# Router logits of two token blocks on VectorE instead of TensorE, in a fused Mamba, MLP and mixture-of-experts kernel

## The chip, the cores and the metric

The kernel runs on one core of one Trainium2 chip. The metric is the device time of one execution in microseconds (us). A core has five engines that work side by side, each with its own queue of instructions, issued in a fixed order: TensorE (PE in the profile; PEld is its loading of weights), VectorE (DVE), ScalarE (ACT), GpSimd (POOL) and SyncE (SP), which here only starts transfers (DMAs). An instruction waits for semaphores of others, and what stands behind it on the same engine waits with it.

## What is computed

The reference takes 2048 tokens of 512 numbers, in float32. A layer norm, an RMS norm, a Mamba-2 layer and an MLP of width 2048 with residuals come first. Then a mixture of experts works on the layer-normed rows; of that part this is what matters here:

```
x = x + attn_and_mlp(layernorm(x))
n = layernorm(x)                                   # (2048, 512)
router_logits = n @ Wr                             # Wr: (512, 8)
topk_w, topk_idx = top_k(softmax(router_logits), 2)
combine = topk_w / sum(topk_w), spread over the 8 experts
y[e] = (silu(n @ Wg[e]) * (n @ Wu[e])) @ Wd[e]     # Wg, Wu: (512, 352), Wd: (352, 512)
out = x + sum over e of combine[e] * y[e]
```

## The kernel before

Tokens lie in 16 tiles of 128 rows. The Mamba layer goes through them in 8 steps of 256 tokens, the MLP (`feed_forward(fb)`) in 4 blocks of 512 tokens, `fb` 0 to 3, each with 16 chunks `c` of 128 hidden channels. From the third Mamba step on, the program interleaves the MLP of one block with the Mamba layer of a later one; the third block's MLP ends after the Mamba layer, and the last block's MLP (`feed`, from 1065 us) runs with the third block's routing and with the loading of all experts' weights into SBUF. Then come the expert tiles.

**The order.** From the third Mamba step on, a region called `manual_schedule` holds PE to the order in which the Python program emits its instructions. The order on the other engines, SP's queue of loads too, is laid down by a scheduler when the kernel is built, by priorities and by its own idea of times; on the chip it is fixed. Generators cut the work into pieces, and each `yield` is a place at which the emitting program goes over to another generator. In the loop over `feed` (`for n in range(4 * NFC)`) four steps make one chunk, and the third step of each chunk (`n % 4 == 2`) is followed by one piece of the routing of block 2 and then of the first table. In the loop over the expert tiles two pieces come with each tile, taken from the routing of block 3 and then from the second table.

**Buffers.** A tile that is allocated with a `tag` shares that tag's `bufs` buffers with all others of the tag, and its first writer waits until one is free. `mid` (3 buffers of 512 numbers for each partition) serves the routing; `mg` (3) and `md` (4) hold MLP weights; `row` (5) the rows of a block; `h2T` one transposed block. In PSUM, `tr`, `g`, `u` and `d` have two banks each from the last block's MLP on.

**The weights of the MLP.** For each chunk SP loads `mg` (L534), `ms` (L547) and `md` (L552); the experts' weights come by L924, L926 and L927. Each waits for its buffer in SP's queue.

**Routing a block** (`route`). When the block's MLP has ended, `normed(j)` writes the normed rows `xn` of tile `j` (L598) and stores them to DRAM in `xnd` (L599), and for blocks 0 to 2 also in `xnd1` (L601), from where the expert tiles gather them later. PE turns each tile of `xn` with four transposes (L201), ACT copies the result to `xT` (L203), and PE multiplies it with the router weights (L607):

```
xT = mid([NK, P], f"xT{fb}_{j}")
transposed(xn, xT)
...
nc.tensor.matmul(pl, xT[:, k, :], wr_sb[:, k, :], start=(k == 0), stop=(k == NK - 1))
```

DVE copies the logits to `lg` (L608) and, when all four tiles are there, picks the two best experts (`chosen`, `both`), their weights, and the counts `prior` of earlier tokens (L627 to L650). Two pieces later PE counts positions with the matmul `pr` (L654, L655), which reads `both` and `prior`, and GpSimd scatters token numbers and weights into `lists` (L669).

**Expert tiles.** `table` makes from `lists` which expert and which tokens each tile of 128 places has. The first table has `NS1` tiles, all full, from blocks 0 to 2 alone; the second has the rest. For tile `s`, GpSimd gathers rows (L1026), PE transposes them and multiplies with the expert's weights (L1045), DVE makes `eh` (L1050) and copies its transpose to `ehT` (L1059), PE multiplies again (L1066), DVE weighs the rows (L1071) and GpSimd adds them to `out` in DRAM (L1072). Rows are fetched up to two tiles ahead.

Of the kernel before, what the change touches and what calls it, by code (L numbers as in the profile page):

```python
# [9 lines left out]
F32 = mybir.dt.float32  # L10
I32 = mybir.dt.int32
AF = mybir.ActivationFunctionType
ALU = mybir.AluOpType
# [3 lines left out]
P = 128  # L17
T = 2048
D = 512
NK = D // P  # L20
# [8 lines left out]
NFB = T // FB  # L29
# [5 lines left out]
NE = 8  # L35
# [3 lines left out]

NS = (2 * T + NE * (P - 1)) // P  # L40

NS1 = 10


NSA = (2 * T + NE * (P // 2)) // P
# [6 lines left out]


@with_exitstack
def mamba_mlp_moe(ctx, tc, x, w_in, w_out, w_gu, w_down, par, wr, wg, wu, wd, out):

    nc = tc.nc

    def bc(ap, axis, n):
        ap = ap.unsqueeze(axis)
        shape = list(ap.shape)
        shape[axis] = n
        return ap.to_broadcast(shape)
# [7 lines left out]
    pmlp = ctx.enter_context(tc.tile_pool(name="pmlp", bufs=2, side="right"))  # L73
    wk = ctx.enter_context(tc.tile_pool(name="wk", bufs=2, side="right"))
# [21 lines left out]
    def load_w_in(pair):  # L96
# [15 lines left out]
        out=tri, in_=ones, pattern=[[1, P]], compare_op=ALU.is_ge, fill=0.0, base=0, channel_multiplier=-1  # L112
# [3 lines left out]
        out=late, in_=ones, pattern=[[-1, P]], compare_op=ALU.is_gt, fill=0.0, base=0, channel_multiplier=1  # L116
# [16 lines left out]
        out=upto, in_=ones[:, : NE * NE].rearrange("p (e f) -> p e f", e=NE), pattern=[[1, NE], [-1, NE]],  # L133
# [27 lines left out]
    xnd = scratch.tile([T + P, D], F32, name="xnd", tag="xnd")  # L161
# [15 lines left out]
    def bank(kind, shape, name):  # L177
        pool, tag = use[kind]
        return pool.tile([P, *shape], F32, name=name, tag=tag)
# [17 lines left out]
    def transposed(src, dst, weight=None, kind="tr"):  # L197

        pt = bank(kind, [NK, P], "pt")
        for k in range(NK):  # L200
            nc.tensor.transpose(pt[:, k, :], src[:, k * P : (k + 1) * P], ident)  # L201
        if weight is None:
            nc.scalar.copy(dst, pt)  # L203
        else:
            nc.vector.tensor_tensor(dst, pt, bc(weight, 2, P), ALU.mult)
# [174 lines left out]
    h2T = [None] * NFB  # L380
# [179 lines left out]
    def mid(shape, name):  # L560
        return wk.tile([P, *shape], F32, name=name, tag="mid", bufs=3)

    NJ = FB // P
    more_rows = None
    mlp_w = None
    newest = None
    NHI = P // NE
    zero = row("zero")
    nc.gpsimd.memset(zero, 0.0)
# [16 lines left out]
    def route(fb, rows):  # L586

        mv2, rs2 = small("mv2", NJ, 2), small("rs2", NJ)
        for j in range(NJ):
            stats(small_p, rows[j], mv2[:, j, :])  # L590
        rsqrt_eps(rs2, mv2[:, :, 1])
        lg, l2, tmp = (small(n, NJ, NE) for n in ("lg", "l2", "tmp"))

        def normed(j):
            t = fb * NJ + j
            nc.scalar.dma_start(out=out[t * P : (t + 1) * P, :], in_=rows[j])
            xn = mid([D], f"xn{t}")
            nc.vector.tensor_scalar(xn, rows[j], mv2[:, j, 0:1], rs2[:, j : j + 1], ALU.subtract, ALU.mult)  # L598
            nc.scalar.dma_start(out=xnd[t * P : (t + 1) * P, :], in_=xn)  # L599
            if fb < NFB - 1:  # L600
                nc.scalar.dma_start(out=xnd1[t * P : (t + 1) * P, :], in_=xn)  # L601
            return xn

        def logits(j, xT):
            pl = bank("d", [NE], f"pl{fb}_{j}")
            for k in range(NK):
                nc.tensor.matmul(pl, xT[:, k, :], wr_sb[:, k, :], start=(k == 0), stop=(k == NK - 1))  # L607
            nc.vector.tensor_copy(lg[:, j, :], pl)  # L608

        xn = normed(0)  # L610
        yield
        for j in range(NJ):
            if j:
                logits(j - 1, xT)
            xT = mid([NK, P], f"xT{fb}_{j}")
            transposed(xn, xT)
            if j < NJ - 1:
                xn = normed(j + 1)
            yield
        logits(NJ - 1, xT)  # L620

        chosen = [small(n, NJ, NE) for n in ("o1", "o2")]
        m1, m2, *mr = (small(n, NJ) for n in ("rm1", "rm2", "mr1", "mr2"))

        def top(src, mx, mr, oh):

            nc.vector.tensor_reduce(mx, src, AX.X, ALU.max)  # L627
            nc.vector.tensor_tensor(tmp, src, bc(mx, 2, NE), ALU.is_equal)
            nc.vector.tensor_tensor(tmp, tmp, bc(rank, 1, NJ), ALU.mult)
            nc.vector.tensor_reduce(mr, tmp, AX.X, ALU.max)  # L630
            nc.vector.tensor_tensor(oh, tmp, bc(mr, 2, NE), ALU.is_equal)

        top(lg, m1, mr[0], chosen[0])
        nc.vector.scalar_tensor_tensor(l2, chosen[0], -3.0e38, lg, ALU.mult, ALU.add)
        top(l2, m2, mr[1], chosen[1])

        wt = [small(n, NJ) for n in ("wt1", "wt2")]
        nc.vector.tensor_tensor(m2, m2, m1, ALU.subtract)
        nc.scalar.activation(m2, m2, AF.Exp)
        nc.vector.tensor_scalar_add(wt[0], m2, 1.0)  # L640
        nc.vector.reciprocal(wt[0], wt[0])
        nc.vector.tensor_tensor(wt[1], m2, wt[0], ALU.mult)


        both, prior = small("both", NJ, NE), small("prior", NJ, NE)
        nc.vector.tensor_tensor(both, *chosen, ALU.add)
        nc.vector.tensor_copy(prior[:, 0, :], before)
        for j in range(1, NJ):
            nc.vector.tensor_tensor(prior[:, j, :], prior[:, j - 1, :], both[:, j - 1, :], ALU.add)
        nc.vector.tensor_tensor(before, prior[:, NJ - 1, :], both[:, NJ - 1, :], ALU.add)  # L650
        yield
        yield
        pr = bank("tr", [NJ, NE], f"pr{fb}")
        nc.tensor.matmul(pr, tri, both, start=True, stop=False)  # L654
        nc.tensor.matmul(pr, ones, prior, start=False, stop=True)  # L655
        nc.vector.tensor_copy(prior, pr)

        for n in range(2):

            at, to = small("at", NJ), small_p.tile([P, NJ], I32, name=f"to{n}", tag=f"to{n}")  # L660
            nc.vector.tensor_tensor(tmp, chosen[n], prior, ALU.mult)
            nc.vector.tensor_reduce(at, tmp, AX.X, ALU.add)
            nc.vector.scalar_tensor_tensor(at, mr[n], -float(T), at, ALU.mult, ALU.add)
            nc.vector.tensor_scalar_add(at, at, NE * T - 1.0)
            nc.vector.tensor_copy(to, at)
            entry = entries[:, n, fb * NJ : (fb + 1) * NJ, :]
            nc.vector.tensor_copy(entry[:, :, 1], wt[n])
            for j in range(NJ):
                nc.gpsimd.indirect_dma_start(  # L669
                    out=writers.pop(), out_offset=bass.IndirectOffsetOnAxis(ap=to[:, j : j + 1], axis=0),  # L670
                    in_=entry[:, j, :], in_offset=None,
                )
            yield
# [117 lines left out]
    for _ in range(3):  # L791
        hT = next(coming)
# [96 lines left out]
    for b in range(NB):  # L889
        fb, at = divmod(b, BPF)  # L890
# [110 lines left out]
    def routed(steps):  # L1001

        nonlocal first
        yield from steps
        first = yield from table(NS1, "1")

# [12 lines left out]
    def of(s):  # L1019

        return (s, first, xnd1) if s < NS1 else (s - NS1, rest, xnd)

# [11 lines left out]
        return xT  # L1034

    def hidden(s, xT):
        n, (exp_i, _, _, _), _ = of(s)
        e = nc.tensor.value_load(exp_i[0:1, n : n + 1], min_val=0, max_val=NE - 1)
        w = ew[:, bass.DynSlice(e, 1), :].rearrange("p a n -> p (a n)")
        pg = bank("g", [EI], f"epg{s}")  # L1040
        pu = bank("u", [EI], f"epu{s}")
        for k in range(NK):
            for a, ps in enumerate((pg, pu)):
                lo = (2 * k + a) * EI
                nc.tensor.matmul(ps, xT[:, k, :], w[:, lo : lo + EI], start=(k == 0), stop=(k == NK - 1))  # L1045
            if k == 1:
                yield
        h = mid([EI], f"eh{s}")
        nc.scalar.activation(h, pg, AF.Silu)
        nc.vector.tensor_tensor(h, h, pu, ALU.mult)  # L1050
        return h, w

    def turned(s, h):

        pt = bank("tr", [len(ET), P], f"pht{s}")
        for m, (lo, n) in enumerate(ET):
            nc.tensor.transpose(pt[:n, m, :], h[:, lo : lo + n], ident)
        hT = wk.tile([P, len(ET), P], F32, name=f"ehT{s}", tag="a", bufs=4)
        nc.vector.tensor_copy(hT[:, 0:2, :], pt[:, 0:2, :])  # L1059
        nc.scalar.copy(hT[: EI - 2 * P, 2, :], pt[: EI - 2 * P, 2, :])  # L1060
        return hT

# [16 lines left out]
    got, xT = {}, {}  # L1079

    def fetch(upto):

        for s in range(min(upto + AHEAD, NSA if rest else NS1)):
            if s not in got:
# [27 lines left out]
    def second():  # L1112

        nonlocal rest
        yield from feed
        rest = yield from table(NS - NS1, "2", first[-1])

# [6 lines left out]
    with tc.If(filled > NSA - NS1):  # L1124
        for s in range(NSA, NS):
            h, w = finish(hidden(s, front(s, gather(s))))
# [67 lines left out]
```

## Time and profile before

| | |
|---|---|
| time, three runs | 1541.31, 1541.85, 1543.73 us; median 1541.85 |
| the profiled execution | 1540.27 us, of which the span of the trace is 1538.6 |
| busy in the span | PE 97%, PEld 66%, DVE 49%, ACT 48%, POOL 28% |
| third block's routing | xn from 1067.2 us, last logits 1119.3, `pr` 1138.2 |
| first table's indices `idx` | 1210.2 us |
| last block's routing | xn from 1231.2 us, last logits 1255.2, `pr` 1263.1 |
| second table's indices | 1294.6 us |
| expert tiles on PE | from 1227.6 us, 8.1 us for each in the middle |

The profile is of one execution, so sums are made against that execution's 1540.27 us. "Busy" counts an engine's instructions; a wait of PE is what lengthens the whole, as PE is busy nearly all the time.

### The profile page before, as it was taken

Reading aid. Unit: us, or ns where it says so; the run is one execution under the profiler, and the core shown is the slowest. Engines: PE = TensorE matmul, PEld = TensorE weight load, DVE = VectorE, ACT = ScalarE, POOL = GpSimd, SP = SyncE. Lnnn points to the kernel's source line nnn. Section 1 sums busy time; section 2 is a strip of 40 time slices with the busy share of each in tenths; the row PEclk is TensorE's granted clock in tenths of the full one; section 3 lists DMA queues with packets and bytes.
Section 4 is the critical chain, followed back from the end, with each engine's and each line's share of the span. In section 5 each row is a group of like instructions: output and inputs, shape, how many; then the busy total and the mean of one; then the engine's idle time right before and its main releaser. Section 6 shows DMA issues by size and latency. Waiting matters only on the chain. (4 is left out here: it accounts for less than half of the span.)

```text
span 1538.6 us, 18825 instructions
## 1 busy us (share of the span) xinstructions
PE 1498.3 (97%) x6153; PEld 1021.0 (66%) x6153; DVE 749.8 (49%) x1939; ACT 744.0 (48%) x1332; POOL 425.5 (28%) x537
## 2 busy tenths in 40 slices
PE   8899999999999999999999999999999999999996
PEld 7566577677667676767676677666776666566553
DVE  7776775645645564556454643334343433222221
ACT  5888967635663598458745754222221231111110
POOL 4432324424242212141212120411131124233321
PEclk9999999999999999999999999999999999999999
DMA  9444445545544554454335532426879434333332
GB/s 305 137 138 125 137 140 183 190 149 171 171 151 148 185 165 131 137 118 157 121 123 179 167 121 89 93 93 209 289 205 260 152 91 64 66 69 65 66 63 35
DMA packets 128241, 217.54 MB, mean 141 GB/s; under 512 B 12560, under 2 KB 72848, under 8 KB 128144
## 3 DMA queue, kind: packets, MB, share of 16 engines
q1 hardware_dynamic: 105376, 166.34, 35.6%
q0 software_dynamic: 9088, 18.91, 7.2%
q10 hardware_dynamic: 13680, 31.07, 5.4%
q8 instruction: 52, 0.85, 0.2%
q14 instruction: 45, 0.37, 0.1%
HBM read 175.48 MB, written 40.80 MB: 141 GB/s over the span
## 5 line engine op out<-in xcount | busy, mean ns | idle before, releaser
L691 PE MATMUL pd<-md,a 128*128 128x512 f32 x512 | 238.8, 593 | 0.8 <-DVE r L692 0.7
L340 PE MATMUL pm<-hT,wi 128*128 128x256 f32 x768 | 185.4, 386 | 3.7 <-DMA wi<-in_w_in 3.7
L340 PEld LDWEIGHTS pm<-hT,wi 128*128 128x128 f32 x768 | 141.7, 192 | 29.2 <-issue 7.9
L692 DVE TENSOR_TENSOR r<-r,pd 128x512 f32<-128x512 f32 x128 | 87.4, 684 | 150.6 <-PE pd L691 149.9
L691 PEld LDWEIGHTS pd<-md,a 128*128 128x128 f32 x512 | 96.9, 190 | 76.6 <-issue 65.8
L361 DVE SCALAR_TENSOR_TENSOR ca<-pre,params,ca 128x256 f32<-128x256 f32 x288 | 143.9, 557 | 0.3
L707 PE MATMUL py<-h2T,ms 128*128 128x256 f32 x512 | 131.7, 380 | 3.5 <-DMA ms<-late 2.6
L772 POOL TENSOR_TENSOR a<-a,up 128x256 f32<-128x256 f32 x64 | 47.0, 734 | 265.7 <-DVE up L766 225.8
L340 PE MATMUL pz<-hT,wi 128*128 128x256 f32 x512 | 117.0, 381 | 0.0
L490 PE MATMUL po<-w_o,zs 128*128 128x512 f32 x256 | 116.2, 607 | 0.0
L1045 PE MATMUL epg<-ew,xgT 128*128 x288 | 109.0, 460 | 0.2 <-ACT xgT L203 0.2
L1045 PE MATMUL epu<-ew,xgT 128*128 x288 | 108.7, 459 | 0.0
L707 PEld LDWEIGHTS py<-h2T,ms 128*128 128x128 f32 x512 | 95.4, 190 | 19.5 <-issue 2.3
L420 ACT ACT_TABLE_LOAD x75 | 96.2, 1283 | 21.5 <-DVE ncum L285 14.5
L340 PEld LDWEIGHTS pz<-hT,wi 128*128 128x128 f32 x512 | 94.8, 190 | 13.8 <-ACT zs L373 0.8
L1066 PE MATMUL epd<-ew,ehT 128*128 (+1 forms) x216 | 98.9, 593 | 1.0 <-DVE ehT L1059 1.0
L420 ACT ACTIVATE cum<-cum,ncum 128x128 f32<-128x128 f32 x256 | 85.7, 392 | 6.2 <-POOL cum L314 4.8
L490 PEld LDWEIGHTS po<-w_o,zs 128*128 128x128 f32 x256 | 49.5, 195 | 58.4 <-issue 57.3
L752 ACT COPY a<-px 128x256 f32<-128x256 f32 x64 | 23.6, 369 | 127.2 <-PE px L707 111.3
L1026 POOL DMA_INDIRECT xg<-xnd,idx x36 | 35.5, 985 | 154.4 <-PE pt L201 150.6
L422 DVE SCALAR_TENSOR_TENSOR cum<-cum,dt,psc 128x128 f32<-128x128 f32 x256 | 72.9, 339 | 5.8 <-PE psc L414 3.6
L203 ACT COPY xgT<-pt 128x512 f32<-128x512 f32 x36 | 21.0, 586 | 111.8 <-PE pt L201 111.8
(240 smaller groups left out, 2528.1 us busy)
## 6 DMA issues: line engine op xcount, KB each, us to landing
wi<-in_w_in SPq DMA_DIRECT2D x80, 512.0 KB, 3.8
ms<-late SPq DMA_DIRECT2D x48, 512.0 KB, 3.7
mg<-early SPq DMA_DIRECT2D x48, 384.0 KB, 3.8
md<-in_w_down SPq DMA_DIRECT2D x64, 256.0 KB, 4.0
cum<-rowsd SPq DMA_DIRECT2D x32, 512.0 KB, 4.1
late<-ms ACTq DMA_DIRECT2D x16, 512.0 KB, 2.7
ec<-rowsd SPq DMA_DIRECT2D x60, 128.0 KB, 3.4
xnd<-xn ACTq DMA_DIRECT2D x28, 256.0 KB, 3.8
```

What stands on the lines that cost most here:

```text
L340: nc.tensor.matmul(pm[:, m, :], w[:, k, m * P : (m + 1) * P], hT[:, k, :], start=(k == 0), stop=(k == NK - 1))
L361: nc.vector.scalar_tensor_tensor(ca, pre[:, m, k : k + TB], cw[:, k : k + 1], ca, ALU.mult, ALU.add)
L420: nc.scalar.activation(lt[:, half, i], lt[:, half, i], AF.Exp, bias=ncum[:, j, h : h + 1])
L422: nc.vector.scalar_tensor_tensor(lt[:, half, i], lt[:, half, i], dt[:, j, h : h + 1], psc[:, half, i], ALU.mult, ALU.mult)
L490: nc.tensor.matmul(po, y[:, m, :], w_o[:, m, :], start=(m == 0), stop=(m == 7))
L691: nc.tensor.matmul(pd, a[:, j * P : (j + 1) * P], d, start=(m == 0), stop=(m == 1))
L692: nc.vector.tensor_tensor(rows[j], rows[j], pd, ALU.add)
L707: nc.tensor.matmul(ps, w[:, k], m[:, k], start=(first and k == 0), stop=(k == KH - 1), skip_group_check=True)
L772: nc.gpsimd.tensor_tensor(a[:, 1], a[:, 1], up, ALU.mult)
L1026: nc.gpsimd.indirect_dma_start(out=xg, out_offset=None, in_=src, in_offset=bass.IndirectOffsetOnAxis(ap=idx[:, n : n + 1], axis=0))
L1045: nc.tensor.matmul(ps, xT[:, k, :], w[:, lo : lo + EI], start=(k == 0), stop=(k == NK - 1))
L1066: nc.tensor.matmul(pd, hT[:n, m, :], w[:n, NG + m * D : NG + (m + 1) * D], start=(m == 0), stop=(m == len(ET) - 1))
```

## The change

Blocks 0 and 1 stay as they are. For the last two blocks PE no longer transposes `xn` for the router and no longer multiplies it. DVE forms each logit as the sum of products of a row with a column of the router weights, which arrives from DRAM copied to all 128 partitions (`wr_rows` is the transposed matrix, a new input). For each block these are 8 experts by 4 tiles, 32 products.

The last block keeps its four normed tiles in SBUF, in the buffer of `h2T`, and loads columns two at a time into buffers of `mg`; its products are queued on DVE behind the latest `eh` or `ehT` of the expert tiles (`turning`). It now has 17 pieces before the choice of experts, where there were five. The third block's normed tiles still go to DRAM through `mid`; they are read back from `xnd` two at a time, also into `mid`, and each column is loaded into `mid`, once for each pair of tiles. Its number of pieces stays the same. The first table has 16 tiles where it had 10.

```diff
-NS1 = 10
+NS1 = 16
...
+        if fb == NFB - 1:
+            kept = wk.tile([P, NJ, D], F32, name="kept", tag="h2T", bufs=1)
...
-            xn = mid([D], f"xn{t}")
+            xn = kept[:, j] if fb == NFB - 1 else mid([D], f"xn{t}")
...
+        def dot(product, xn, col, j, e):
+            nc.vector.scalar_tensor_tensor(
+                product, xn, 1.0, col, ALU.mult, ALU.mult, accum_out=lg[:, j, e : e + 1]
+            )
+
+        if fb == NFB - 1:
+            for j in range(NJ):
+                normed(j)
+                if j % 2:
+                    yield
+            for e in range(NE):
+                if e % 2 == 0:
+                    cols = pmlp.tile([P, 2, D], F32, name=f"cols{e}", tag="mg", bufs=3)
+                    nc.sync.dma_start(out=cols, in_=bc(wr_rows[e : e + 2], 0, P))
+                for j in range(NJ):
+                    with tc.issue_after(turning):
+                        dot(pmlp.tile([P, D], F32, name="dot", tag="md", bufs=4), kept[:, j], cols[:, e % 2], j, e)
+                    if j == 1 or j == 3 and e < NE - 1:
+                        yield
+        elif fb == NFB - 2:
+            for j in range(NJ):
+                normed(j)
+                if j % 2:
+                    yield
+            for j in range(0, NJ, 2):
+                two = []
+                for t in (fb * NJ + j, fb * NJ + j + 1):
+                    two.append(mid([D], f"xb{t}"))
+                    nc.sync.dma_start(out=two[-1], in_=xnd[t * P : (t + 1) * P, :])
+                for e in range(NE):
+                    col = mid([D], f"col{j}_{e}")
+                    nc.sync.dma_start(out=col, in_=bc(wr_rows[e], 0, P))
+                    for n in range(2):
+                        dot(bank("tr", [D], "dot"), two[n], col, j + n, e)
+                    if e % 4 == 3 and j + e < NJ + NE - 3:
+                        yield
+        else:
...
-        nc.vector.tensor_tensor(h, h, pu, ALU.mult)
+        turning = nc.vector.tensor_tensor(h, h, pu, ALU.mult).ins
...
-        nc.vector.tensor_copy(hT[:, 0:2, :], pt[:, 0:2, :])
+        turning = nc.vector.tensor_copy(hT[:, 0:2, :], pt[:, 0:2, :]).ins
```

More of the change, by code (lines that the diff above doesn't have):

```diff
@@ L54, in mamba_mlp_moe @@
 @with_exitstack
-def mamba_mlp_moe(ctx, tc, x, w_in, w_out, w_gu, w_down, par, wr, wg, wu, wd, out):
+def mamba_mlp_moe(ctx, tc, x, w_in, w_out, w_gu, w_down, par, wr, wr_rows, wg, wu, wd, out):
     nc = tc.nc
@@ L566, in mamba_mlp_moe @@
     newest = None
+    turning = None
     NHI = P // NE
@@ L608, in logits @@
             nc.vector.tensor_copy(lg[:, j, :], pl)
[L610 to L618, printed above, removed]
-            yield
-        logits(NJ - 1, xT)
+        def dot(product, xn, col, j, e):
+            nc.vector.scalar_tensor_tensor(
+                product, xn, 1.0, col, ALU.mult, ALU.mult, accum_out=lg[:, j, e : e + 1]
+            )
@@ new lines, in route @@
+        if fb == NFB - 1:
[30 more added lines that the diff above has]
+        else:
+            xn = normed(0)
+            yield
+            for j in range(NJ):
+                if j:
+                    logits(j - 1, xT)
+                xT = mid([NK, P], f"xT{fb}_{j}")
+                transposed(xn, xT)
+                if j < NJ - 1:
+                    xn = normed(j + 1)
+                yield
+            logits(NJ - 1, xT)
@@ L1036, in hidden @@
     def hidden(s, xT):
+        nonlocal turning
         n, (exp_i, _, _, _), _ = of(s)
@@ L1049, in hidden @@
         nc.scalar.activation(h, pg, AF.Silu)
-        nc.vector.tensor_tensor(h, h, pu, ALU.mult)
+        turning = nc.vector.tensor_tensor(h, h, pu, ALU.mult).ins
         return h, w
     def turned(s, h):
+        nonlocal turning
         pt = bank("tr", [len(ET), P], f"pht{s}")
@@ L1178 @@
         "wr": a["Wr"],
+        "wr_rows": a["Wr"].T,
         "wg": a["Wg"],
```

## The prediction

> **What bounds the kernel now.** I read the page first, then what TensorE (PE) waits for, then its order in time around the router, then the queue of SyncE (SP), which issues the loads. Section 1 of the page:
>
> ```profile
> span 1538.6 us, 18825 instructions
> PE 1498.3 (97%) x6153; PEld 1021.0 (66%) x6153; DVE 749.8 (49%) x1939; ACT 744.0 (48%) x1332; POOL 425.5 (28%) x537
> ```
>
> PE is the bound, VectorE (DVE) is half idle. PE's own waits add up to 29 us, and their longest group is this (in total, times, longest):
>
> ```profile
> PE pc L273 <- DVE dA L270: 5.3, 3, 2.9
> ```
>
> So work taken off PE is worth its full length wherever nothing new stops PE. The timeline of PE (start, length, line) prices the removed steps, shows where PE first needs the third block's choice of experts, and what follows a stop:
>
> ```profile
> 34.08 5.38 PE L340 MATMUL pm<-hT,wi 128*128 128x256 f32 x16 [3.71 <-DMA wi<-in_w_in]
> ...
> 44.67 3.62 PE L340 MATMUL pz<-hT,wi 128*128 128x256 f32 x16
> ...
> 1086.05 0.95 PE L607 MATMUL pl<-wr_sb,xT 128*128 128x8 f32 x8
> 1086.86 0.64 PE L201 MATMUL pt<-ident,xn 128*128 128x128 f32 x4
> 1087.33 1.03 PE L707 MATMUL px<-ts,ms 128*128 128x256 f32 x4
> ...
> 1138.17 0.30 PE L654 MATMUL pr<-both,tri 128*128 128x32 f32 x2
> ```
>
> From start to start one tile's logits cost 0.81 us and its transposes 0.47. The matmul pr stands at 1138.2 us in an order that is written out by hand: if its input is late, all of PE stands still there. The same 16 matmuls took 5.38 us after a wait of 3.71 and 3.62 us when PE ran on: a stop of that length costs another 1.8.
>
> **What is removed.** Eight tiles (four of each block) lose 0.81 + 0.47 = 1.28 us on PE: 10.2 us, 5.1 in each block. The eight copies of xT on ScalarE (0.58 each) and of lg on DVE (0.16) go too; both engines have idle time there, so nothing is counted for them.
>
> **What is added for the last block.** 32 products on DVE and four loads of 512 KB. The nearest row for a product is the three-operand instruction of the same shape at L499:
>
> ```profile
> L499 DVE SCALAR_TENSOR_TENSOR h<-po,ry,h 128x512 f32<-128x512 f32 x16 | 12.0, 751 | 0.7
> ```
>
> I take 0.75 us and 0.05 for the sum that it also writes, 0.8; with a separate read as on ScalarE (L504, 0.19 us) it would be 0.94, and by the two-operand row of this shape (L692) 0.68. Two products come with each half of an expert tile, four per tile. PE needs 8.1 us per tile; DVE does 1.7 us now (eh 0.52, ehT 0.42, ey 0.75) and would do 4.9. The products stand behind the last eh or ehT copy in DVE's order, and PE does half a tile (some 2.4 us of matmuls) before it needs either, against 1.6 us of a pair. Rows stay in SBUF and columns have three buffers, which the feed forward has left by then. Hidden; uncovered, each pair could cost PE at most 1.6 us, 26 us in all. The second table comes later by some 12 half tiles: 28 steps of 4.05 us after about 1229 us give 1342, and tile 16, the first that needs it, is fetched as tile 14 begins, 1229 + 14 x 8.1 = 1342. From the table's matmul to the transposes of tile 16 there is over a tile, 8 us, against some 6 (1.3 for idx, 1.0 for the gather, 3.4 to land). The larger NS1 covers it; nothing is counted. So this block brings 5.1 us.
>
> **What is added for the third block.** Everything goes through the tag mid, which has three buffers. Two hold rows, so one is left for columns: the load of a column waits for both products of the column before, and they wait for the load. Sixteen columns (eight for each pair of tiles) stand in one chain, and pr waits for the last of them. SP issues 20 loads of 256 KB (5.2 MB) amid the weights. What a load takes to land, from the page's DMA issues (KB, median us):
>
> ```profile
> md<-in_w_down SPq DMA_DIRECT2D x64, 256.0 KB, 4.0
> cum<-rowsd SPq DMA_DIRECT2D x32, 512.0 KB, 4.1
> r<-resd SPq DMA_DIRECT2D x16, 256.0 KB, 3.5
> ```
>
> and for md between 1065 and 1135 us alone, where experts' weights are loaded ahead of it and DMA is 0.7 to 0.97 busy:
>
> ```profile
> DMA to landing us min/median/max: 5.1/6.8/7.6
> ```
>
> SP is not free either. In 1065 to 1205 us it stands in two waits of the weights for 82 of 140 us:
>
> ```profile
> SPq L547 <- PE px L707: 41.5, 13, 4.8
> SPq L534 <- PE px L707: 40.5, 13, 4.3
> ```
>
> A column behind one of these is late; weights behind a column's wait are late too. In the trace ms is issued 10.5 us before its use (1094.4 against 1105.0) and lands in some 4, so 6.5 us may be lost there before PE feels it.
>
> Start: the scales are there at 1067.2 us. Three normed rows fill mid by 1069; their two stores each, landing in 3.0 to 5.6 us, free the first buffer at about 1074; the fourth row is stored by 1076 and frees its buffer at about 1081. The first column starts then.
>
> One column while PE runs: 0.1 us from release to issue, 1.0 for SP's place in its queue (59% of waits that last 3.2 us), 4.0 to land (between r and md, nearer r), 0.1, two products 1.6, 0.3 behind other work of DVE: 7.1. With PE standing still the rest is quiet: 0.1 + 2.9 (the shortest md and ec are 2.7) + 0.1 + 1.6 = 4.7. Here the Trainium skill speaks for a cheaper load: "DMA: Bandwidth & Descriptors", section "Anatomy of one DMA — SWDGE (gpsimd) path", gives 2.0 us and the bytes at 436 GB/s, so 2.6 us for a column (an estimate from the page, whose fit is for the other path). By it all columns take 4.4. By the rows above only the shortest loads come near, so I use the rows and keep 4.4 as the lower end; the upper is 8.5 for all (md's 6.8 to land, 1.7 of work).
>
> Sum: without the router's work PE reaches pr at 1138.2 - 5.1 = 1133.1. Seven columns at 7.1 from 1081 end at 1131. Nine at 4.7 add 42, changing rows between the pairs 1.5 (two more issues of 0.35 and a busier landing): 1174.5. From lg to prior DVE has 14 small operations; in this trace 1119.5 to 1124.1 with 1.1 of other work inside, so 3.5: pr at 1178, 40 later than now. The scatters of the lists, the first table and its gathers follow at their old distance in PE's order. Then 1.8 for the stop and -5.1 for the last block: +36.5. By the page's load: 1081 + 16 x 4.4 + 1.5 + 3.5 = 1156, +18 at pr, +15 in all. By the upper end: 1081 + 136 + 5 = 1222, +84 at pr, +81.
>
> This is against the profiled execution, whose time is 1540.3 (span 1538.6); the median of the three runs, 1541.85, is 1.6 higher. 1541.85 + 36.5 = 1578; with some allowance for weights held up behind columns, 1580.
>
> **Rivals.**
>
> *The chain is hidden, PE only gains.* Then 1541.85 - 10.2 = 1532. For it: PE at 97%, DVE at half. Against: the chain has 1133 - 3.5 - 1.5 - 1081 = 47 us, 2.9 per column, and the shortest load (2.7) with two products (1.6) already takes more. It holds only if two columns are in flight, that is if a fourth buffer or an earlier release exists; mid's "bufs=3" speaks against. Chance 0.08.
>
> *A short chain.* Columns come from one 2 KB row and land near the shortest seen, and SP's order puts them well: 4.4 to 5 us each, +15 to +24: 1557 to 1566. For: the 128 KB broadcast ec landed in 2.7 at best. Against: ec's median is 3.4 and DMA is busy there. Chance 0.25.
>
> *The likeliest*, one wait at pr of 30 to 55 us: 1567 to 1597. Chance 0.42.
>
> *Lock step.* The orders of SP and DVE are fixed, so weights wait behind columns and DVE's sums of the feed forward behind products that have no column yet; PE then goes at the chain's pace and the chain at PE's, 8 us and more a column: 1597 to 1625. For: SP's 59% of waits. Against: 6.5 us of lead in ms. Chance 0.23. No change at all is left with 0.02: it needs gain and wait to cancel.
>
> **How the numbers follow.** A difference of 0.2% (3.1 us) is about what a measurement of this kernel can tell from none. Faster 0.08, within 0.2% 0.02, slower 0.9 (0.25 + 0.42 + 0.23). The range leaves out the gain, the lowest of the short chains and the upper part of lock step: 1555 to 1612.
>
> **What would show it.** In the changed profile: rows L607 with half as many matmuls; a wait of PE at pr for DVE's both or prior of some 40 us between 1130 and 1190, and the granted clock below 1 after it; SP's waits of columns on DVE's products one after another, 4.5 to 7 us apart; the DMA issues with 16 columns at 3 to 5 us to landing; the expert tiles at 8.1 us each with no router matmuls between them, ending on PE without new waits. I am wrong if pr starts before 1140 (columns overlapped), if a product takes over 1 us, if PE waits in the expert tiles for ehT or for the second table, or if most of the wait is for ms and mg before pr.

## The result

| | median us | runs | ratio to before |
|---|---|---|---|
| before | 1542.79 (1541.31 to 1546.03) | 4 | |
| changed | 1594.14 (1590.78 to 1596.05) | 4 | 1.0318 [1.0296, 1.0340] |

The change makes the kernel 51 us slower, 3.2%. The forecast was 1580 with a range of 1555 to 1612.

### The profile after

The head of the page answers to the one shown of before:

```profile
span 1594.3 us, 18779 instructions
PE 1506.9 (95%) x6057; PEld 1021.4 (64%) x6057; DVE 782.0 (49%) x2059; ACT 740.0 (46%) x1324; POOL 428.3 (27%) x537
```

PE has 96 records fewer than before and is nevertheless busy 8.6 us longer (1506.9 against 1498.3). What was taken away did go; something made the rest slower. The waits of PE say where it stood (in total, times, longest):

```profile
PE pr L700 <- DVE both L692: 18.7, 1, 18.7
PE py L753 <- DVE a L786: 16.6, 6, 7.0
...
PE py L753 <- DMA ms<-late: 4.0, 1, 4.0
PE px L753 <- DVE up L812: 3.2, 1, 3.2
```

The wait at `pr` that the forecast names is there, but it is only 18.7 us. About as much again, 19.8 us, is spread over the last block's feed forward: its matmuls wait for DVE's sums `a` and `up`, with which the router has nothing to do. DVE's order in time shows why (start, length, wait before it). The first column comes late, its two products stand ahead of the sum L786 in DVE's fixed order, and DVE waits 10.36 us with the sum behind it:

```profile
1097.98 0.70 DVE L616 SCALAR_TENSOR_TENSOR dot<-xb,col 128x512 f32<-128x512 f32 x1 [10.36 <-DMA col<-in_wr_rows]
...
1099.85 0.41 DVE L786 TENSOR_TENSOR a<-a,py 128x256 f32<-128x256 f32 x1
```

PE in the same stretch, then where it reaches `pr`, and after it:

```profile
1092.26 1.03 PE L753 MATMUL px<-h2T,ms 128*128 128x256 f32 x4
1100.31 2.08 PE L753 MATMUL py<-h2T,ms 128*128 128x256 f32 x4 [7.03 <-DVE a L786]
...
1169.57 2.07 PE L753 MATMUL py<-h2T,ms 128*128 128x256 f32 x4 [2.39 <-DVE a L786]
...
1190.37 0.64 PE L700 MATMUL pr<-both,tri 128*128 128x32 f32 x2 [18.73 <-DVE both L692]
...
1214.93 2.04 PE L753 MATMUL py<-h2T,ms 128*128 128x256 f32 x4 [3.98 <-DMA ms<-late]
```

Four matmuls of this kind take 1.03 us ahead of a stop and 2.0 to 2.1 behind one. The granted clock in short stretches (window, length, then PE, PEld, DVE, ACT, POOL busy, then the clock, the share of DMA and GB/s): behind the waits of 7.03, 2.39, 18.73 and 3.98 us, and once ahead of the second:

```profile
1100.30:1104.00 3.70, 3.69 (x9) 2.97 (x10) 0.29 (x1) 0.41 (x1) 0.73 (x1) 0.50 0.72 204
...
1160.00:1169.50 9.50, 7.17 (x27) 4.75 (x25) 4.22 (x12) 1.12 (x3) 1.34 (x3) 1.00 0.83 254
1169.50:1171.60 2.10, 2.04 (x4) 1.17 (x4) 0.34 (x2) 0.42 (x1) 0.73 (x1) 0.51 0.54 203
...
1190.40:1194.00 3.60, 3.60 (x9) 2.74 (x10) 2.85 (x22) 0.00 (x0) 0.66 (x1) 0.50 0.00 0
1194.00:1198.00 4.00, 4.00 (x10) 2.20 (x9) 1.03 (x3) 0.17 (x1) 3.08 (x4) 0.64 0.40 101
...
1215.00:1219.00 4.00, 4.00 (x10) 3.19 (x11) 0.64 (x2) 0.42 (x1) 0.00 (x0) 0.50 1.06 324
```

So behind each of these stops PE runs at half the clock for a while, here for some 3 to 6 us unless the next stop cuts it short. Now the chain itself, by the products and their columns (ns min/median/max, first and last start):

```profile
L616 DVE SCALAR_TENSOR_TENSOR dot<-xb,col x32: 689/701/733, 1098.0 to 1186.8; 128x512 f32<-128x512 f32 x32
L616 DVE DVE_READ_ACCUMULATOR dot<-xb,col x32: 136/141/144, 1098.6 to 1187.5; 128x1 f32 x32
L650 SPq DMA_DIRECT2D col<-in_wr_rows x16: 327/328/382, 1092.7 to 1183.1; - x16
...
  DMA col<-in_wr_rows: 44.6, 14
...
DMA to landing us min/median/max: 3.0/3.7/5.9
```

DVE stood 44.6 us for columns. The last three follow each other while PE stands:

```profile
1177.10 0.70 DVE L616 SCALAR_TENSOR_TENSOR dot<-xb,col 128x512 f32<-128x512 f32 x1 [3.13 <-DMA col<-in_wr_rows]
...
1181.67 0.70 DVE L616 SCALAR_TENSOR_TENSOR dot<-xb,col 128x512 f32<-128x512 f32 x1 [3.17 <-DMA col<-in_wr_rows]
...
1186.21 0.70 DVE L616 SCALAR_TENSOR_TENSOR dot<-xb,col 128x512 f32<-128x512 f32 x1 [3.13 <-DMA col<-in_wr_rows]
```

One every 4.55 us: two products, then a load that could not start before them.

### Where the 51 us are

Two profiled executions of one kernel can already differ ahead of the change: the last tile's output projection starts at 1020.9 us in the first profile of before, at 1029.3 in a second one, at 1028.3 in the changed kernel. So stages are compared, not positions.

| stage | before | before, second profile | changed |
|---|---|---|---|
| output projection of the last tile to `pr` of the third block | 117.3 | 117.2 | 162.1 |
| `pr` to the first expert matmul | 90.7 | 91.7 | 98.4 |
| expert matmuls to the end | 309.7 | 310.7 | 305.5 |

PE up to `pr`, behind it, and in the first two stages together, before:

```profile
1020.90:1138.20 117.30, 115.54 (x460) 81.17 (x459) 46.34 (x110) 32.41 (x70) 13.94 (x31) 1.00 0.66 221
1138.20:1228.90 90.70, 87.88 (x331) 59.99 (x329) 36.74 (x100) 16.65 (x43) 18.79 (x35) 1.00 0.73 201
1020.90:1228.90 208.00, 203.43 (x789) 141.16 (x787) 83.08 (x210) 49.06 (x113) 32.73 (x65) 1.00 0.69 213
```

The same, changed:

```profile
1028.30:1190.40 162.10, 119.47 (x412) 79.34 (x410) 65.12 (x163) 29.32 (x66) 15.91 (x31) 0.89 0.61 194
1190.40:1288.80 98.40, 94.12 (x331) 64.15 (x331) 37.72 (x108) 17.55 (x43) 18.34 (x34) 0.93 0.69 199
1028.30:1288.80 260.50, 213.59 (x742) 143.49 (x740) 102.84 (x270) 46.86 (x109) 34.26 (x65) 0.91 0.64 196
```

The two stages take 52.5 us more. PE stands 46.9 us instead of 4.6 (260.50 - 213.59 against 208.00 - 203.43), which is +42.3; it has 5.1 less to do and is yet busy 10.2 longer, so the matmuls that are left take 15.3 longer. Of these 15.3 us, 9.0 lie ahead of `pr` (119.47 against 115.54 less 5.1) and 6.2 behind it (94.12 against 87.88, with as many records). The granted clock, read in half-microsecond windows, accounts for some 12.7 of them (an estimate: busy time times what the clock lacks, 6.8 ahead of `pr` and 5.9 behind); the rest stays open. The expert stage gives 4.2 back. Sum +48.3; the medians say +51.4, and single runs of one kernel spread over 5 us.

As a sum this is right, but the parts ahead of `pr` are not costs of their own. When `pr` can start is set by the chain: PE stood 18.7 us there, and without the earlier stops and the slower clock it would have stood longer. What lengthens the kernel is 44.8 us up to `pr` (162.1 against 117.3) and 7.7 behind it (6.7 against the second profile of before): 6.2 of slower matmuls and 1.5 more of standing, for late `ms` above all. How far the chain itself would run faster beside a faster PE, no run separates.

### The profile page after: what moved, and what is told of

The parts are those of the page before. It is cut to its first block, busy times and chain, and to the rows that moved or that the text cites. A ratio compares the mean times of both kernels' runs of the same rounds, so it can differ in the third digit from the quotient of the medians.

```text
span 1594.3 us, 18779 instructions
## 1 busy us (share of the span) xinstructions
PE 1506.9 (95%) x6057; PEld 1021.4 (64%) x6057; DVE 782.0 (49%) x2059; ACT 740.0 (46%) x1324; POOL 428.3 (27%) x537
## 5 line engine op out<-in xcount | busy, mean ns | idle before, releaser
L737 PE MATMUL pd<-md,a 128*128 128x512 f32 x512 | 243.6, 603 | 2.6 <-DVE r L738 2.5
L340 PE MATMUL pm<-hT,wi 128*128 128x256 f32 x768 | 188.7, 391 | 4.8 <-DMA wi<-in_w_in 4.8
L753 PE MATMUL py<-h2T,ms 128*128 128x256 f32 x512 | 136.9, 391 | 21.3 <-DVE a L786 16.6
L361 DVE SCALAR_TENSOR_TENSOR ca<-pre,params,ca 128x256 f32<-128x256 f32 x288 | 140.4, 545 | 0.3
L1092 PEld LDWEIGHTS epu<-ew,xgT 128*128 128x128 f32 x288 | 54.7, 190 | 30.5
```

The lines of the kernel that those rows point to most:

```text
L340: nc.tensor.matmul(pm[:, m, :], w[:, k, m * P : (m + 1) * P], hT[:, k, :], start=(k == 0), stop=(k == NK - 1))
L361: nc.vector.scalar_tensor_tensor(ca, pre[:, m, k : k + TB], cw[:, k : k + 1], ca, ALU.mult, ALU.add)
L737: nc.tensor.matmul(pd, a[:, j * P : (j + 1) * P], d, start=(m == 0), stop=(m == 1))
L753: nc.tensor.matmul(ps, w[:, k], m[:, k], start=(first and k == 0), stop=(k == KH - 1), skip_group_check=True)
```

## The experiments

Theory: in the third block one buffer of `mid` is left for columns, so load and products take turns, and PE pays for that chain in waits and in clock. Rivals: SP's queue of 20 more loads makes weights late; the products' own time; or the last block loses too. Each ratio below is to the kernel before, run again beside the experiment, with its interval. The medians of before were 1548.5 to 1549.8 us there, not 1542.8, so an expectation in us is to be read by its distance to before.

**The last block alone.** The third block's logits go back to PE.

```diff
-        elif fb == NFB - 2:
+        elif fb == NFB:
```

> Only the last block's logits on VectorE (16 tiles in the first table), the third block's on TensorE as before. Chain theory (the one free buffer of the third block's columns costs all of the loss): 5 us less than before, about 1538, as the expert stage in the trace of the change was 4.2 us shorter. Rival (the whole change costs time, in the expert stage too, or the 7 us that the changed kernel lost ahead of the third block's routing come with the new program): 1543 to 1550.

Measured 0.9973 [0.9956, 0.9990], that is 4.2 us less; the expert stage is 305.6 us as in the changed kernel. The waits of its expert stage hold nothing above 1.0 us:

```profile
PE epd L1114 <- DVE ehT L1107: 1.0, 2, 0.5
PE pht L1105 <- DVE eh L1097: 0.7, 1, 0.7
PE epd L1114 <- issue: 0.6, 1, 0.6
```

The last block's half of the change does what it should, and its 32 products are hidden.

**The third block alone.** The last block back on PE, `NS1 = 10`.

> Only the third block's logits on VectorE, the last block's on TensorE as before (10 tiles in the first table). Chain theory: the loss alone, 4 to 5 us above the changed kernel, 1597 to 1600. Rival (the two blocks disturb each other): clearly below the changed kernel's 1594.

Measured 1.0353 [1.0320, 1.0386], 55 us more, as the chain theory expected. The loss is all in the third block; PE waits 19.7 us at `pr` and 18.4 for the sums `a`.

**Two buffers for columns.** The same 20 loads, 32 products and queues; only the columns go to a tag with two buffers free.

```diff
-                    col = mid([D], f"col{j}_{e}")
+                    col = row(f"col{j}_{e}")
```

> The changed kernel, but the third block's columns alternate between two buffers that are idle until the expert tiles; the same 20 loads in the same queue and the same 32 products. Chain theory: a column comes every (0.1+3.7+0.1+1.7)/2 to 3.7 us where it was 5.9, so the 16 take 45 to 60 us and pr's wait goes; between 1535 and 1552. Rival (the number of loads in SyncE's queue holds up the weights): little changes, 1580 or more. Rival (the products on VectorE hold up the feed forward's sums): the waits of TensorE for VectorE's a stay, some 15 us, with 1550 to 1560.

Measured 1.0045 [1.0033, 1.0058]. One more buffer takes 42 us away of the 49 that the ratio 1.0318 stands for (1.0318 - 1.0045 = 0.0273). A column takes 3.6 us on the mean instead of 5.9, as expected, and PE no longer waits at `pr`. PE's stretch from the output projection to the experts, with the same 742 records:

```profile
1028.30:1246.60 218.30, 201.80 (x742) 136.47 (x740) 102.28 (x270) 46.63 (x109) 36.46 (x65) 0.99 0.74 234
```

It stands 16.5 us instead of 46.9, and the same matmuls take 11.8 us less at a clock of 0.99 instead of 0.91. That the number of loads on SP sets the time is excluded: it is the same here. (Outside `mid` the first columns need not wait for the rows' stores either, but the first product starts only 3.8 us earlier.) For what is left, the rival of the products holds: 10.5 of the 16.5 us are waits for DVE.

```profile
PE py L753 <- DVE a L786: 4.3, 2, 2.9
PE pd L737 <- DVE dot L616: 3.1, 1, 3.1
PE px L753 <- DVE up L812: 3.1, 2, 2.9
```

**The columns issued by ScalarE.**

```diff
-                    nc.sync.dma_start(out=col, in_=bc(wr_rows[e], 0, P))
+                    nc.scalar.dma_start(out=col, in_=bc(wr_rows[e], 0, P))
```

> The changed kernel with the third block's 16 column loads issued by ScalarE instead of SyncE; rows and weights stay with SyncE. Chain theory: still one buffer, still 16 links of 5 to 6 us, ratio 1.025 to 1.04; ScalarE's own sums may wait behind a load's wait, which makes it no better. Rival (SyncE's queue is what is held up): half of the loss or more goes, below 1.016.

Measured 1.0349 [1.0330, 1.0368], no better. The chain is as long (`pr` 164.9 us after the output projection), a column lands later (median 4.9 us instead of 3.7), and now ScalarE's copies stand behind a column's wait (in the whole run):

```profile
PE pr L700 <- DVE both L692: 15.0, 1, 15.0
...
PE px L753 <- ACT a L805: 11.1, 4, 5.5
PE py L753 <- DVE a L786: 10.0, 4, 3.0
```

So the chain does not need a place in SP's queue to be as long: that place is not the cause.

**`pr` one piece later.** A `yield` more ahead of `pr` in the third block.

> The changed kernel with one more empty piece ahead of the third block's position matmul, which so stands one chunk, 9.5 us of TensorE work, later in TensorE's order. If the chain ends at a fixed time and TensorE only waits there: 8 to 10 us less than the changed kernel, ratio about 1.026, unless the first expert tile then waits for its indices. Rival (TensorE and the chain pace each other through VectorE, so that chunk runs at the chain's pace too or pushes it back): 0 to 4 us less, 1.029 or more.

Measured 1.0269 [1.0247, 1.0290]: the chain ends where it did (`pr` 164.2 us after the output projection) and its wait falls from 18.7 to 10.6, since PE has one more piece of feed forward to do ahead of it. The 8 us are those 8; the waits for `a` stay (16.5). So work that PE gets done in that wait does not move the chain's end.

**One product for each column.** First with one row of each pair left unused:

```diff
-                    for n in range(2):
-                        dot(bank("tr", [D], "dot"), two[n], col, j + n, e)
+                    dot(bank("tr", [D], "dot"), two[0], col, j, e)
+                    nc.vector.tensor_copy(lg[:, j + 1, e : e + 1], lg[:, j, e : e + 1])
```

> The changed kernel with one product for each column of the third block; the logit of the pair's second tile is a copy of the first's (0.16 us), so 256 tokens are routed by the logits of others. Chain theory: each of 16 links is shorter by 0.84 - 0.16 = 0.65 to 0.7 us, 10 to 11 us less in all: about 41 us over before, ratio 1.026. Rival (loads set the pace and products lie beside them): no change, 1.032 or more.

Half of the third block's logits are left out here. Measured 1.0349 [1.0331, 1.0367], which answers another question than the one asked. The row without a reader gave its buffer to the columns: they come every 3.3 us, and `pr` stands 132.6 us after the output projection instead of 162.1. But the other choice of experts lengthens the expert stage to 346 us, so the total says nothing. With both rows in use (`n = e % 2`) the question could be put again:

> As the change, but each column of the third block is multiplied with one of the two tiles, in turn, and the logit is copied to the other tile: both rows stay in use, so one buffer is left for columns as in the change, and a column has one product (0.70 us and 0.14 for its sum) instead of two. Left out: half of the third block's logits, so its choice of experts differs and the number of tiles per expert may too; only the time up to pr is read. If load and products follow each other in one chain, a column takes some 0.7 less: 5.2 us on the mean instead of 5.9, 3.9 with PE standing instead of 4.55, and pr stands some 11 us earlier against the last tile's output projection (151 us after it instead of 162). If only the loads set the pace, nothing changes there (162). If VectorE's place behind other work sets it, 155 to 160.

In one profile, `pr` stands 152.5 us after the output projection, 9.6 earlier. A column takes 5.24 us on the mean (first products 1101.0 to 1179.6, 15 steps) instead of 5.88, and 3.9 to 4.1 with PE standing:

```profile
1171.59 0.70 DVE L616 SCALAR_TENSOR_TENSOR dot<-xb,col 128x512 f32<-128x512 f32 x1 [0.69 <-DMA col<-in_wr_rows]
...
1175.46 0.70 DVE L616 SCALAR_TENSOR_TENSOR dot<-xb,col 128x512 f32<-128x512 f32 x1 [2.93 <-DMA col<-in_wr_rows]
...
1179.57 0.70 DVE L616 SCALAR_TENSOR_TENSOR dot<-xb,col 128x512 f32<-128x512 f32 x1 [3.17 <-DMA col<-in_wr_rows]
```

The product that is gone (the second starts 0.62 us behind the first) is in the period in full, 5.88 - 5.24 = 0.64, so load and products stand in one row. With the two buffers this shows the chain from both sides.

**Rows kept in SBUF.** The four normed tiles stay in `mid` and in a spare buffer of `row`; each column is loaded once (8 loads) into `row` and used four times.

```diff
-            for j in range(0, NJ, 2):
-                two = []
...
+            for e in range(NE):
+                col = row(f"col{e}")
+                nc.sync.dma_start(out=col, in_=bc(wr_rows[e], 0, P))
+                for j in range(NJ):
+                    dot(bank("tr", [D], "dot"), four[j], col, j, e)
```

> The third block's four normed rows stay in SBUF (three buffers of mid and the spare one of row), each column is loaded once, into two buffers idle until the expert tiles: 8 loads where there were 20, the same 32 products. Chain theory: hidden, the 10 us gain of TensorE show: 1532 to 1537. Rival (products hold up the sums): 10 to 20 us above that.

Measured 1.0011 [0.9997, 1.0024], no gain, in the lower part of the rival's range. The chain no longer holds up PE: there is no wait at `pr`, and DVE waits 8.4 us for columns where it waited 44.6. Yet none of the 5.1 us that the block takes off PE comes through: PE stands 12.0 us in the two stages (4.0 in the kernel with the last block alone), 4.3 of it still for the sums `a`.

**The same with the products placed.** Products are laid behind the last sum of a chunk (`issue_after(swept)`), in sixes, the pieces go behind the fourth step of a chunk instead of the third, and there is one piece less ahead of `pr`. So more than the products' place changes here.

```diff
+                    with tc.issue_after(swept):
+                        dot(bank("tr", [D], "dot"), four[j], col, j, e)
...
-        if n % 4 == 2:
+        if n % 4 == 3:
```

> As the rows-kept version (8 loads into two buffers, 32 products), but each group of six products is queued on VectorE behind the last sum of a chunk of the feed forward, where VectorE has some 5 us until the next sum that TensorE waits for; the choice of experts comes one piece later and its position in TensorE's order stays within a chunk. Theory (the 12 us that the rows-kept version still loses in this block are products that stand ahead of the sums): the loss goes, 8 to 10 us faster than before, ratio 0.994. Rival (the 8 loads in SyncE's queue hold up the weights): as the rows-kept version, ratio 1.000 to 1.002. Rival (VectorE simply has too little time): no better than 1.000.

Measured 0.9982 [0.9968, 0.9995], less than the gain expected (0.994). The waits for `a` are gone in the two stages; PE stands 8.7 us there, mostly for this:

```profile
PE py L756 <- DMA ms<-late: 5.2, 4, 3.1
```

**Stores, then columns too, issued by GpSimd.** Two steps on from it:

```diff
-            nc.scalar.dma_start(out=xnd[t * P : (t + 1) * P, :], in_=xn)
+            store = nc.gpsimd if fb == NFB - 2 else nc.scalar
+            store.dma_start(out=xnd[t * P : (t + 1) * P, :], in_=xn)
```

> As the kernel with the rows kept and the products placed behind the last sum of a chunk, but the eight stores of the third block's normed rows are issued by GpSimd instead of ScalarE, so that ScalarE's copies for the feed forward don't stand behind them. If those stores make the waits that are left (8.7 us of PE standing between the output projection and the first expert matmul, 4.6 in the kernel before), they fall to 5 to 6, and the time is 2 to 3 us less than with the stores on ScalarE: ratio to before 0.996 to 0.9965. If the waits are those of late weights, whose loads have another order on SP, nothing changes: 0.998.

> As the kernel before this one, and the eight loads of columns of the third block are issued by GpSimd too, so that SP has the weights alone. If columns in SP's queue make ms late (5.2 us of PE's waits in the kernel with the products placed, 2.6 before), PE stands 4 to 5 us in the stage as before, and both blocks' gain comes through, 7 to 9 us: ratio 0.994 to 0.9955. If ms is late for another reason, as the kernel before this one: 0.996 to 0.998.

Measured 0.9990 [0.9975, 1.0004] and 0.9967 [0.9953, 0.9982]. The second is 5.1 us less than before, but no better than the last block alone by these intervals. What was expected of the queues did not come: PE stands 10.4 and 11.0 us in the two stages, and with SP left to the weights it waits for late `ms` more, not less, and for `mg` too:

```profile
PE py L757 <- DMA ms<-late: 7.3, 2, 5.9
PE px L757 <- DMA mg<-early: 2.1, 1, 2.1
```

These waits are of one profile each. So columns in SP's queue are not what makes `ms` late; what does stays open. Nor are the 5.1 us a gain of the third block, by that profile: its two stages take 213.8 us, 5.8 more than before.

```profile
1029.00:1242.80 213.80, 202.77 (x742) 137.91 (x740) 103.63 (x270) 46.88 (x109) 47.43 (x81) 0.98 0.74 225
```

It is the end that is shorter there, 7.2 us from PE's last matmul to the end of the span, against 10.7 before, 10.9 with the last block alone and 11.4 with only the stores on GpSimd. Why is not known.

**The kernel before, a second time.**

> The kernel before, a second profiled execution. In its first profile the last tile's output projection starts at 1021 us, in those of the change and of all its variants at 1027 to 1030, though nothing is changed ahead of it. If that is scatter between executions or between placements, it comes anywhere from 1020 to 1030 here, with the stage from there to the first expert matmul at 208 us as before. If the change itself slows the early stages (another order on some engine), it comes at 1021 again.

Its output projection of the last tile starts at 1029.3 us, and from there to the experts it takes 208.9 us. So a start as late as in the changed kernel comes without the change too, and the 8 us need not be due to it. One more execution says no more than that.

## Why the prediction was right, and where its sizes were off

| step | forecast | measured |
|---|---|---|
| last block | -5.1 | -4.2 [-6.8, -1.5] |
| first column issued, after the output projection (1020.9 then) | 60.1 | 64.4 |
| 16 columns, first issue to the last product's end | 93.5 | 94.9 |
| one column with PE standing / running | 4.7 / 7.1 | 4.55 / 6.2 |
| last logit to `pr` | 3.5 | 2.8 |
| `pr` after the output projection | 157.1 | 162.1 |
| PE stands more in the two stages | 45 | 42.3 |
| same matmuls longer, ahead of `pr` / behind it | 0 / 1.8 | 9.0 / 6.2 |
| `pr` to the experts, more than before | 1.8 | 7.7 |
| both blocks together | +36.5, 38 with the allowance | +48.3 in the profiles, +51 in the medians |

The median lies in the likeliest case (1567 to 1597), near its upper end. That is in part luck: this case was one wait at `pr` of 30 to 55 us, and the wait there is 18.7; the rest came by other ways. The sign that was named for it, some 40 us at `pr`, did not show.

*Mechanism.* One buffer, load and products in turn, 16 columns, `pr` late: right, and shown by the two buffers (-42 us) and by the single product (-9.6). The chain's length is right to 2 us, partly by two errors: running columns were faster than forecast (12 of them from the first product at 1098.0 to 1172.6, 6.2 each), and only some three columns, not nine, fell in PE's stop at `pr`.

*The terms that were mis-sized.* From the forecast's +36.5 to the +48.3 in the profiles 11.8 us are missing. Up to `pr` they are 5.0 (162.1 against 157.1): the first column comes 4.3 late, since the rows' stores landed in 5.8 to 7.6 us where 3.0 to 5.6 were taken; the chain is 1.4 longer, the choice of experts 0.7 shorter. SP's wait ahead of the first column, then the landing of those stores:

```profile
SPq L650 <- DMA xnd<-xn: 2.7, 1, 2.7
```

```profile
DMA to landing us min/median/max: 5.8/6.7/7.6
```

Behind `pr` they are 5.9: the forecast put 1.8 for one stop on top of the old distance, and it is 7.7. The matmuls behind the stops at `pr` and at the late `ms` take 6.2 longer, and PE stands 1.5 longer. The last 0.9 are the expert stage (4.2 less, where 5.1 were counted).

*One wait or many.* The forecast put the whole wait at one place. It is cut into the wait at `pr` and eight others ahead of it, of 1.2 to 7.0 us, and behind six stops, of 2.4 us and more (four of them ahead of `pr`), PE ran at half the clock. Ahead of `pr` its matmuls took 9.0 us longer, which the forecast does not have. They are not missing in its sum: they fill time in which PE would else have stood at `pr`.

*Why the wait was cut up.* Of the lock-step rival one half came true: DVE's sums stood behind products that had no column. The other half did not: PE waited 4.0 us for late weights, where before it waited 2.6 (that columns held them up is not shown), and the column's pace was 6 us, not 8. The forecast kept these as two cases with a chance each; parts of both came together.

*The load.* By the Trainium skill, "DMA: Bandwidth & Descriptors", section "Anatomy of one DMA — SWDGE (gpsimd) path", a column would land in 2.6 us (an estimate from its fit, which is for the other path). It took 3.0 at best and 3.7 at the median here; the rows of the trace (2.9 and 4.0 in the forecast) were the better guide.

*The clock's rule.* The Trainium skill, "TensorE: Matmul & The Clock Gate", "Part 1: The HAM clock gate", says that the array goes to half rate after an idle window of some 3.4 us and comes back after about as long a busy one. By it the three waits above 3.4 us would cost 1.7 each, 5.1 in all (an estimate from the page). The half rate behind the wait of 2.39 us, from a clock of 1.00, shows that a shorter stop was enough here. But 2.4 us is no threshold either. One stop of the feed forward lasts 2.63 us in the trace of every run, ahead of the change; here before and changed:

```profile
848.47 1.13 PE L707 MATMUL px<-h2T,mg 128*128 128x256 f32 x4 [2.63 <-DVE a L771]
```

```profile
852.79 2.07 PE L753 MATMUL px<-h2T,mg 128*128 128x256 f32 x4 [2.63 <-DVE a L817]
```

Behind it the clock fell to half in 11 of the 14 traces and stayed up in three. Counting in these traces the stops that began at full clock with no other stop close behind, none of 25 between 1.2 and 1.5 us was followed by half the clock, 55 of 88 between 1.5 and 3.1, and all 31 of more. So over a range of lengths the same stop may or may not cost the clock.

*The last block* was costed right in kind: 0.69 for a product and 0.08 for its sum, where 0.75 and 0.05 were taken, no new wait among the expert tiles.

*The gain that was counted on.* The forecast subtracted the third block's 5.1 us of PE's work as sure wherever no new wait comes. Without the chain, new waits came all the same, and none of the four placements of these products is better than the last block alone. In the kernel with the products placed, PE is busy 4.7 us less than with the last block alone (198.9 against 203.7) and stands 4.6 longer (8.7 against 4.0). The waits for the sums (4.3 us) went when the products were placed, together with the shift of the pieces, so these two are not told apart. Of the weights that come late after that, it is known only that the columns' place in SP's queue is not the cause.

## What to carry to other kernels

Count the buffers of a tag, subtract what lives long, and see what is left for what streams: with one left, load and use take turns, and the count times their sum is a floor. An engine with idle time is not free work when its order is fixed: an instruction that waits for a transfer holds up everything behind it, and the bound engine waits for that. When a chain on other engines decides when the bound engine can go on, its stops and its slower clock ahead of that point fill the wait for it; what comes behind that point is to be priced on top. A stop of TensorE of 1.5 to 3.1 us was followed by half the clock in some cases here, a longer one in all, for some 3 to 6 us.

## What was not expected of the hardware

A product with a summed output leaves two records on DVE: 0.70 us and a read of the accumulator of 0.14 us, which overlaps the next product (the second starts 0.62 us after the first). In the last block, with the product written to SBUF rather than PSUM, they are 0.685 and 0.081:

```profile
L616 DVE SCALAR_TENSOR_TENSOR dot<-kept,cols x32: 683/685/691, 1299.9 to 1358.2; 128x512 f32<-128x512 f32 x32
L616 DVE DVE_READ_ACCUMULATOR dot<-kept,cols x32: 80/81/85, 1300.6 to 1358.8; 128x1 f32 x32
```

A column's issue takes 0.56 us on GpSimd against 0.33 on SP.
